# Wide one-hots of the counts, for eight groups of edges at a time, in a graph network kernel

## The chip, the cores and the metric

The kernel runs on one core of one Trainium2 chip. The metric is the device time of one execution in microseconds; the time of a kernel is the median of several runs. The engines of a core are named as in the profile: PE (TensorE, matrix products), with PEld for its loads of weights; DVE (VectorE); ACT (ScalarE); POOL (GpSimd, here the engine that issues gathers and scatters); SP (SyncE, here the engine that issues plain transfers). Each engine runs its own instructions in order and waits for the others by semaphores.

## The reference

A graph with 6,250 nodes of 256 features and 100,000 edges goes through four message-passing layers. The edges come sorted by `dst`.

```python
h = jnp.maximum(_layernorm(x, axis=-1), 0.0)      # the input of the network
def agg(h):
    return jax.ops.segment_sum(h[src], dst, num_segments=N)
x1 = h
for l in range(NL - 1):                            # three layers
    g = x1 + agg(x1)
    g = jax.nn.relu(g @ W1s[l] + b1s[l])
    g = jax.nn.relu(g @ W2s[l] + b2s[l])
    x1 = g @ W3s[l] + b3s[l]
g = x1 + agg(x1)                                   # the head
g = jax.nn.relu(g @ cW1 + cb1)
g = jax.nn.relu(g @ cW2 + cb2)
return x + g @ cW3 + cb3
```

## The kernel before

The 6,250 nodes are `NT` = 49 blocks of 128. The sum over edges is a matrix product: for a block of 128 destination nodes a matrix of counts (source nodes x 128 destinations, entries "so many edges from here to there") multiplies the feature rows. The counts are small, so a matrix is kept as bytes, and the product `agg` (L1928) takes it block by block of sources, with the features split into a rounded part and a remainder (`XY`, two matmuls for each half of the features). The matrices depend on the edges alone: they are built once, during layer 0, stored to memory (`mats`) and read again by the later layers. `BUILT` = 32 destination blocks ("slots") have such a matrix. The other work of a layer, up to 19 blocks of destinations, goes by gathers: POOL fetches rows of the feature table by index (L1613) and DVE adds them up (`sums`, L1649; the first pair of rows of a block is copied by ACT, L1645). Behind either comes the small network of the layer (L1408, L1505).

**How counts are built.** 32 slots x 2 halves x 4 make 256 *units*, one more for a long block. A unit (`BATCH` = 4 groups of 128 edges; a group has at most 128 edges, one a partition, whose destinations are four neighbouring nodes) makes two one-hots in bfloat16:

- `lo`, 128 x (4 x 128): for each edge, a 1 at the lane of its source node within a block. One DVE operation for the four groups (L1197), which compares `lanes` with the edges' codes. The codes are held doubled in `pairs` (each twice, side by side), a copy that ACT makes for 16 groups at a time (L1190).
- `hi`, 128 x (4 x 98): for each edge, at the column of its source block (49 blocks x 2), a weight. The two columns of a block hold a 16-bit number each, that is two counts of a byte; the weight says which byte the edge adds to. Four DVE operations, one a group (L1215): compare `cols` with the edge's column code and multiply by its weight, both scalars of the partition, read from `marks`, float32 copies that ACT makes for 16 groups at a time (L1192).

PE multiplies `lo` by `hi` group by group (L1245, four matmuls into `bp`), and ACT (now and then DVE) casts `bp` into `at`, the bytes of the slot (L1253, L1255); SP stores a finished slot (L1261).

**What sets the order.** The program is written out in order by Python generators, with no scheduler behind it. `build` yields once a unit. The first `PRE` = 28 units (three slots and four units) are built alone, between them the steps of `listed`, which sorts the blocks of nodes and, with `at` of L1728, makes the list of edges that POOL fetches (L1734) for the gathers. Six of its steps are one-hot products of their own (L1702, L1706, L1711 on DVE, L1718 on PE). Then `product` runs over panels of up to four slots and 49 blocks of sources; at each step it emits the DVE and ACT work that is due, units of `build` by a table of goals (`goals`, about one a step at first), and the four `agg` matmuls, whose operand `a` is cast from bytes by ACT or DVE some steps ahead (L1896 to L1901). While unit k is emitted, `lo` and `hi` of unit k + 1 are emitted ahead of it, and the codes of the unit four further on. `lo`, `hi` and `bp` have two buffers each, so `lo` of unit k + 1 waits for the matmuls of unit k - 1. Gathers are released by time estimates that advance with PE's matmuls (`passed`). Layer 0 ends near 720 us of the span; nothing is built after it.

Of the kernel before, what the change touches and what calls it, by code (L numbers as in the profile page):

```python
# [9 lines left out]
F32 = mybir.dt.float32  # L10
# [4 lines left out]
BF16 = mybir.dt.bfloat16  # L15
AF = mybir.ActivationFunctionType
OP = mybir.AluOpType
PSUM = bass.MemoryType.PSUM
DRAM = bass.MemoryType.DRAM
P = 128  # L20
# [400 lines left out]
def sorted_edges(  # L421
# [39 lines left out]
    nc = tc.nc  # L461
# [10 lines left out]
    GSUB = 64 // GD  # L472
    TWO = GD // 2
    HW = NT * TWO
# [4 lines left out]
    BATCH = 4  # L479
# [52 lines left out]
    clT = const.tile([P, 3, GSUB, 2 * BUILT], BF16, name="clT")  # L532
# [7 lines left out]
    extra = const.tile([P, 3, BATCH], BF16, name="extra")  # L540
    limit = const.tile([P, NS], F32, name="limit")
    mark = const.tile([1, 4], F32, name="mark")
    cT, weigh, loT = clT[:, 0], clT[:, 1], clT[:, 2]
    colf = const.tile([P, P], F32, name="colf")
    cols = const.tile([P, HW], BF16, name="cols")
    lanes = const.tile([P, P], BF16, name="lanes")
# [550 lines left out]
    with tc.manual_schedule():  # L1097
        with tc.tile_pool(name="prep", bufs=2) as prep, tc.tile_pool(
            name="ps_t", bufs=2, space=PSUM
# [67 lines left out]
        batches = []  # L1167
# [5 lines left out]
                batches.append((slot, None, 1, GSUB - BATCH))  # L1173
        hot = {}

        pairs, marks = {}, {}

        def pair(hots, k):

            if k < len(batches):  # L1180
                slot, s, half, q0 = batches[k]
                if s is None:
                    pairs[slot, 2] = hots.tile([P, BATCH, 2], BF16, name="more", bufs=1)
                    nc.vector.tensor_copy(pairs[slot, 2],
                                          extra[:, 2, :, None].to_broadcast([P, BATCH, 2]))
                    marks[slot, 2] = hots.tile([P, 2, BATCH], F32, name="moremarks", bufs=1)
                    nc.vector.tensor_copy(marks[slot, 2], extra[:, :2])
                elif q0 == 0:
                    pairs[slot, half] = hots.tile([P, GSUB, 2], BF16, name="pairs", bufs=3)
                    nc.scalar.copy(pairs[slot, half], loT[:, :, s, None].to_broadcast([P, GSUB, 2]))  # L1190
                    marks[slot, half] = hots.tile([P, 2, GSUB], F32, name="marks", bufs=3)
                    nc.scalar.copy(marks[slot, half], clT[:, :2, :, s])  # L1192

        def one_hot(o, values, which, n):

            shape = [P, BATCH, n // 2, 2]
            nc.vector.tensor_tensor(  # L1197
                o.rearrange("p q (n t) -> p q n t", t=2),
                values.rearrange("p (n t) -> p n t", t=2)[:, None, :, :].to_broadcast(shape),
                which[:, :, None, :].to_broadcast(shape), OP.is_equal)  # L1200

        def low_hot(hots, k):
            if k < len(batches):
                slot, s, half, q0 = batches[k]
                lo = hots.tile([P, BATCH, P], BF16, name="lo", bufs=2)
                one_hot(lo, lanes, pairs[slot, 2] if s is None else pairs[slot, half][:, q0:q0 + BATCH], P)
                hot[k] = [lo]

        def high_hot(hots, k):
            if k < len(batches):  # L1210
                slot, s, half, q0 = batches[k]
                hi = hots.tile([P, BATCH, HW], BF16, name="hi", bufs=2)
                w, o = (marks[slot, 2], 0) if s is None else (marks[slot, half], q0)
                for q in range(BATCH):
                    nc.vector.tensor_scalar(hi[:, q, :], cols, w[:, 0, o + q:o + q + 1],  # L1215
                                            w[:, 1, o + q:o + q + 1], op0=OP.is_equal, op1=OP.mult)
                hot[k].append(hi)

        own_at = [None]

        def build(hots, ats, ps_b):


            each = GSUB // BATCH
            pair(hots, 0)
            low_hot(hots, 0)
            high_hot(hots, 0)
            step, held = 0, None
            for k, (slot, s, half, q0) in enumerate(batches):
                if half == 0 and q0 == 0:  # L1230
                    at = own_at[0] = ats.tile([P, NT, P], U8, name="at", bufs=2)
                more = k + 1 < len(batches) and batches[k + 1][1] is None
                sets = [hot.pop(k)] if held is None else [held, hot.pop(k)]
                pair(hots, k + each)
                if s is not None:
                    low_hot(hots, k + 1)
                    high_hot(hots, k + 1)
                if more:
                    held = sets[0]
                    yield  # L1240
                    continue
                bp = ps_b.tile([P, W], F32, name="bp")
                for m in range(BATCH):
                    for i, (lo, hi) in enumerate(sets):
                        mm = nc.tensor.matmul(bp[:, m * HW:(m + 1) * HW], lo[:, m, :], hi[:, m, :],  # L1245
                                              start=(i == 0), stop=(i == len(sets) - 1))
                passed(SLOW if now[0] < PRE else BUILD * len(sets), mm)
                d = (half * 64 + q0 * GD) // 2
                o = at.bitcast(U16)[:, :, d:d + BATCH * TWO].rearrange("p h (i d) -> p h i d", i=BATCH)
                v = bp[:, :BATCH * HW].rearrange("p (i h d) -> p h i d", i=BATCH, d=TWO)  # L1250
                step += 1
                if step % 8 or step <= PRE:
                    nc.scalar.copy(o, v)  # L1253
                else:
                    nc.vector.tensor_copy(o, v)  # L1255
                if half and q0 + BATCH == GSUB:
                    kind, b = seq[slot]
                    if kind == "u":
                        own = at[:, b - NS, :]
                        nc.vector.tensor_tensor(own, own, ident, OP.add)  # L1260
                    nc.sync.dma_start(out=mats[slot // 4][:, slot % 4, :],  # L1261
                                      in_=at.rearrange("p h d -> p (h d)"))
                if s is None:
                    held = None
                    low_hot(hots, k + 1)
                    high_hot(hots, k + 1)
                yield

        CH = 7
# [602 lines left out]
        def passed(t, ins=None):  # L1872

            clock[0] += t
            if ins is not None:
                paced[:] = [ins.ins.name]
                for g in layers:
                    g.flow()
# [85 lines left out]
        with tc.tile_pool(name="hots", bufs=1) as hots, tc.tile_pool(  # L1964
            name="ats", bufs=1
        ) as ats, tc.tile_pool(name="rings", bufs=AHEAD + 2) as rings, tc.tile_pool(
            name="gath", bufs=9
        ) as gath, tc.tile_pool(name="nd", bufs=1) as nd, tc.tile_pool(
            name="ps_a", bufs=2, space=PSUM
        ) as ps_a, tc.tile_pool(name="ps_b", bufs=2, space=PSUM) as ps_b:  # L1970
            begun = {0: clock[0]}
            beside = build(hots, ats, ps_b)
            lists = listed(nd, ps_b)
            while now[0] < PRE:
                next(beside)
                built[0] += 1
                next(lists, None)
                tick(layers[0])
                layers[0].advance()
                if built[0] == UNITS * (FIRST - 1) + 3:  # L1980
                    at = chunks.tile([P, 4, CH * P], U8, name="at", bufs=5)
                    nc.sync.dma_start(out=at[:, :FIRST - 1, :], in_=mats[0][:, :FIRST - 1, :CH * P])
                if built[0] == UNITS * FIRST:
                    mat[0, 0] = [(at[:, :FIRST - 1, j * P:(j + 1) * P], own_at[0][:, j, :])
                                 for j in range(CH)]
                    for _ in range(2):
                        fetch(0, 0)
            for p in range(last[0] + 1):
                product(0, p, ps_a, beside)
            assert next(beside, None) is None and built[0] == total  # L1990
            assert next(lists, 0) == 0
# [14 lines left out]
def kernel(  # L2006
# [27 lines left out]
    rest = (x, src, dst, W1s, b1s, W2s, b2s, W3s, b3s, cW1, cb1, cW2, cb2, cW3, cb3, out)  # L2034
    earlier = []
    sorted_edges(tc, good, earlier, *rest)
    done = nc.values_load(good[0:1, 0:1], min_val=0, max_val=1)
    with tc.If(done == 0):
# [27 lines left out]
```

## Time and profile before

| What | Value |
|---|---|
| Median of 3 runs | 2024.81 us (2024.36 to 2026.46) |
| The profiled execution | 2030.06 us |
| Its span, first to last instruction | 2028.2 us |
| PE busy | 1909.6 us, 94% |
| DVE busy | 1118.4 us, 55% |
| `hi`, L1215, 1024 operations | 250.7 us of DVE |
| `lo`, L1197, 256 operations | 107.0 us of DVE |

All times of the trace are of one profiled execution, counted from the start of its span. A row of the page's slices has 40 digits, one for 50.7 us each, in tenths of busy time. In a timeline, a row is the start, the duration, the engine, the line and operation, what is written and read with the sizes, and in brackets how long the engine was idle before it and whose work ended that; neighbouring rows of one kind are merged (x4), with the duration from the start of the first to the end of the last. In a table of stretches each engine has its busy time and, behind it, the number of instructions, then the granted clock of PE (1.00 is full), the share of the DMA engines, and GB/s. A row of the list of waits gives who waited for whom, the total in microseconds, how often, and the longest.

### The profile page before, as it was taken

To read this page: it belongs to the slowest core of one execution; us is meant where nothing else is said; L and a number is where in the kernel's file an instruction comes from. 1 tells how busy PE (TensorE), PEld (TensorE's weight loads), DVE (VectorE), ACT (ScalarE), POOL (GpSimd) and SP (SyncE) were. 2 spreads that over 40 slices of the span, in tenths; PEclk is the share of its full clock that TensorE was granted. 3 is DMA by queue.
4 is the path that set the end of the run, shared out by engine and by line. 5 is a ranking of instruction groups with operands and counts; after the bars stand their busy time and mean duration, and the time that the engine had idled before them with its cause. 6 is when DMAs were issued, how large, how long until landed. Compare 5 with 4: busy or idle time off the path is not lost. (4 is left out here: it accounts for less than half of the span.)

```text
span 2028.2 us, 29980 instructions
## 1 busy us (share of the span) xinstructions
PE 1909.6 (94%) x9236; PEld 1477.3 (73%) x9236; DVE 1118.4 (55%) x2984; ACT 1080.1 (53%) x2228; POOL 1304.6 (64%) x1444
## 2 busy tenths in 40 slices
PE   5856999999999899999999999999999999999997
PEld 3643667677777777777789777777789777777765
DVE  7779989898876634334344443333335344443433
ACT  4634667676676555444444564444445464454442
POOL 2525556666766637677777656776777466777775
PEclk9876999999999999999999999999999999999998
DMA  5513546666656746556556675555557576665553
GB/s 167 172 59 121 166 148 210 198 203 188 208 175 192 227 151 191 171 180 184 170 174 189 195 225 172 169 169 179 179 173 214 160 233 191 197 190 178 181 174 106
DMA packets 252342, 361.47 MB, mean 178 GB/s; under 512 B 33353, under 2 KB 206313, under 8 KB 252155
## 3 DMA queue, kind: packets, MB, share of 16 engines
q1 hardware_dynamic: 188160, 190.34, 29.7%
q0 software_dynamic: 61952, 166.87, 27.6%
q10 hardware_dynamic: 2058, 2.25, 0.4%
q8 instruction: 74, 1.21, 0.3%
q14 instruction: 98, 0.79, 0.1%
HBM read 292.33 MB, written 67.40 MB: 177 GB/s over the span
## 5 line engine op out<-in xcount | busy, mean ns | idle before, releaser
L1928 PE MATMUL agg<-a,XY 128*128 128x512 f32 (+1 forms) x6272 | 1510.7, 393 | 16.0 <-DVE a L1901 9.6
L1613 POOL DMA_INDIRECT rows<-table,idxN x1121 | 1084.0, 967 | 493.5 <-PE agg L1928 205.8
L1928 PEld LDWEIGHTS agg<-a,XY 128*128 128x128 f32 x6272 | 1144.3, 189 | 254.6 <-issue 15.0
L1899 ACT CAST a<-at 128x512 fp32r<-128x512 uint8 (+1 forms) x1249 | 707.4, 601 | 239.6 <-PE agg L1928 228.9
L1649 DVE TENSOR_TENSOR sums<-sums,rows 128x512 f32<-128x512 f32 x477 | 333.1, 698 | 483.9 <-DMA rows<-table,idxN 441.7
L1215 DVE TENSOR_SCALAR hi<-cols,marks 128x98 bf16<-128x98 bf16 x1024 | 250.7, 326 | 0.0
L1901 DVE CAST a<-at 128x512 fp32r<-128x512 uint8 (+1 forms) x312 | 141.2, 459 | 167.4 <-PE agg L1928 141.9
L1253 ACT CAST at<-bp 128x392 uint16<-128x392 f32 x227 | 111.0, 489 | 144.6 <-PE bp L1245 141.6
L1245 PE MATMUL bp<-hi,lo 128*128 128x98 bf16 x1028 | 118.7, 215 | 34.9 <-DVE hi L1215 31.5
L1245 PEld LDWEIGHTS <-lo 128*128 128x128 bf16 x1028 | 61.3, 100 | 111.1 <-DVE hi L1215 65.7
L1408 PE MATMUL ps<-h,w 128*128 128x512 f32 (+2 forms) x336 | 135.8, 548 | 0.0
L1505 PE MATMUL ps<-w,h 128*128 128x256 f32 x588 | 133.7, 379 | 0.0
L1197 DVE TENSOR_TENSOR lo<-lanes,pairs 128x512 bf16<-128x512 bf16 x256 | 107.0, 418 | 29.7 <-PE bp L1245 25.1
L1505 PEld LDWEIGHTS ps<-w,h 128*128 128x128 f32 x588 | 111.2, 190 | 15.8
L596 POOL DMA_INDIRECT table<-zz,ids x72 | 72.1, 1002 | 68.8 <-DVE zz L1510 48.4
L1645 ACT COPY sums<-rows 128x512 f32<-128x512 f32 x74 | 43.8, 592 | 123.8 <-DMA rows<-table,idxN 93.7
L1411 ACT ACTIVATE h<-ps,bias 128x512 f32<-128x512 f32 (+2 forms) x84 | 51.7, 636 | 96.0 <-PE ps L1408 95.8
L1510 DVE TENSOR_TENSOR zz<-ps,w 128x512 f32<-128x512 f32 (+1 forms) x81 | 50.4, 637 | 94.5 <-PE ps L1505 87.5
L1408 PEld LDWEIGHTS ps<-h,w 128*128 128x128 f32 x336 | 63.1, 193 | 52.4 <-issue 37.3
L1684 ACT ACTIVATE h<-pt,bias 128x256 f32<-128x256 f32 (+1 forms) x84 | 33.1, 446 | 126.6 <-PE pt L1676 125.3
L1335 DVE TENSOR_TENSOR XY<-back,XY 128x256 fp32r<-128x256 f32 x138 | 54.1, 421 | 42.5 <-ACT XY L1334 41.9
L1942 ACT ACTIVATE h<-agg,bias 128x512 f32<-128x512 f32 (+1 forms) x60 | 37.3, 670 | 73.5 <-PE agg L1928 73.3
(235 smaller groups left out, 889.3 us busy)
## 6 DMA issues: line engine op xcount, KB each, us to landing
at<-mat SPq DMA_DIRECT2D x140, 448.0 KB
mat<-at SPq DMA_DIRECT2D x32, 784.0 KB
at<-mat SPq DMA_DIRECT2D x62, 336.0 KB
rows<-table,idxN POOLq DMA_INDIRECT x1121
back<-table SPq DMA_DIRECT2D x138, 128.0 KB
table<-zz SPq DMA_DIRECT2D x35, 256.0 KB
at<-mat SPq DMA_DIRECT2D x63, 112.0 KB
own<-zz SPq DMA_DIRECT2D x55, 128.0 KB
```

Source lines behind the costliest of these rows:

```text
L596: got = nc.gpsimd.indirect_dma_start(out=ap, out_offset=bass.IndirectOffsetOnAxis(ap=ids[:, b:b + 1], axis=0), in_=sb, in_offset=None)
L1197: nc.vector.tensor_tensor(o.rearrange("p q (n t) -> p q n t", t=2), values.rearrange("p (n t) -> p n t", t=2)[:, None, :, :].to_broadcast( ...
L1215: nc.vector.tensor_scalar(hi[:, q, :], cols, w[:, 0, o + q:o + q + 1], w[:, 1, o + q:o + q + 1], op0=OP.is_equal, op1=OP.mult)
L1245: mm = nc.tensor.matmul(bp[:, m * HW:(m + 1) * HW], lo[:, m, :], hi[:, m, :], start=(i == 0), stop=(i == len(sets) - 1))
L1253: nc.scalar.copy(o, v)
L1408: mm = nc.tensor.matmul(ps[:, :w], weights[l][0][:, c, i * P:(i + 1) * P], h1[:, c, :w], start=(c == 0), stop=(c == KC - 1))
L1505: mm = nc.tensor.matmul(o, h2[0][:, c, nodes], w3[:, c, :], start=(c == 0), stop=(c == KC - 1))
L1613: got = nc.gpsimd.indirect_dma_start(out=t[:, c % 2, :], out_offset=None, in_=tables[self.l][:, :], in_offset=bass.IndirectOffsetOnAxis(ap ...
L1649: nc.vector.tensor_tensor(sums, sums, rows.rearrange("p h c -> p (h c)"), OP.add)
L1899: nc.scalar.copy(o, v)
L1901: nc.vector.tensor_copy(o, v)
L1928: mm = nc.tensor.matmul(agg[c][:, :w], XY[:, j, o:o + P], a[:, :w], start=(i == 0 and half == 0), stop=(i == NT - 1 and half == 1))
```

## The change

`hi` is made for two units, eight groups, at once: one comparison of `cols` with the eight groups' column codes, and one multiplication, in place, by their weights. For this the codes and weights too are held doubled, in one tile with those of `lo`: `pairs` becomes 3 x 16 x 2 in bfloat16 and `marks` goes. `high_hot` is called in every second unit, for the units two and three ahead; it then makes the entry of `hot` to which `low_hot` adds. A helper, `compare`, does all three operations; `of` gives the number of groups: eight, or four for the long block's extra unit.

```diff
         def pair(hots, k):
...
                 elif q0 == 0:
-                    pairs[slot, half] = hots.tile([P, GSUB, 2], BF16, name="pairs", bufs=3)
-                    nc.scalar.copy(pairs[slot, half], loT[:, :, s, None].to_broadcast([P, GSUB, 2]))
-                    marks[slot, half] = hots.tile([P, 2, GSUB], F32, name="marks", bufs=3)
-                    nc.scalar.copy(marks[slot, half], clT[:, :2, :, s])
+                    pairs[slot, half] = hots.tile([P, 3, GSUB, 2], BF16, name="pairs", bufs=3)
+                    nc.scalar.copy(pairs[slot, half],
+                                   clT[:, :, :, s, None].to_broadcast([P, 3, GSUB, 2]))
...
+        def compare(o, values, which, op):
+
+            n, width = o.shape[1], o.shape[2]
+            shape = [P, n, width // 2, 2]
+            o = o.rearrange("p q (n t) -> p q n t", t=2)
+            if values is None:
+                values = o
+            else:
+                values = values.rearrange("p (n t) -> p n t", t=2)[:, None, :, :].to_broadcast(shape)
+            nc.vector.tensor_tensor(o, values, which[:, :, None, :].to_broadcast(shape), op)
...
         def high_hot(hots, k):
             if k < len(batches):
-                slot, s, half, q0 = batches[k]
-                hi = hots.tile([P, BATCH, HW], BF16, name="hi", bufs=2)
-                w, o = (marks[slot, 2], 0) if s is None else (marks[slot, half], q0)
-                for q in range(BATCH):
-                    nc.vector.tensor_scalar(hi[:, q, :], cols, w[:, 0, o + q:o + q + 1],
-                                            w[:, 1, o + q:o + q + 1], op0=OP.is_equal, op1=OP.mult)
-                hot[k].append(hi)
+                codes, o, n = of(k)
+                hi = hots.tile([P, 2 * BATCH, HW], BF16, name="hi", bufs=2)
+                compare(hi[:, :n], cols, codes[:, 0, o:o + n], OP.is_equal)
+                compare(hi[:, :n], None, codes[:, 1, o:o + n], OP.mult)
+                for i in range(n // BATCH):
+                    hot[k + i] = [hi[:, i * BATCH:(i + 1) * BATCH]]
...
                 if s is not None:
                     low_hot(hots, k + 1)
-                    high_hot(hots, k + 1)
+                    if q0 % (2 * BATCH) == 0:
+                        high_hot(hots, k + 2)
```

DVE's order before, in the part built alone, from the last one-hots of `listed` to `at` of L1728 (x4 stands for four equal instructions; a semaphore that is waited for is named in brackets, Activation for ACT):

```order
L1711 TENSOR_TENSOR moved<-block,what 128x576 [waits DVE_49]
L1197 TENSOR_TENSOR lo<-lanes,pairs 128x512 [waits PE_49]
L1215 TENSOR_SCALAR hi<-cols,marks 128x98 x4
L1197 TENSOR_TENSOR lo<-lanes,pairs 128x512 [waits PE_49]
L1215 TENSOR_SCALAR hi<-cols,marks 128x98 x4
L1197 TENSOR_TENSOR lo<-lanes,pairs 128x512 [waits PE_49]
L1215 TENSOR_SCALAR hi<-cols,marks 128x98 [waits DVE_49]
L1215 TENSOR_SCALAR hi<-cols,marks 128x98 x3
L1723 COPY got<-sums 128x144 [waits PE_49]
L1725 SCALAR_TENSOR_TENSOR begin<-got 128x24 [waits DVE_49]
L1728 SCALAR_TENSOR_TENSOR at<-got,begin 128x24 [waits DVE_49]
```

And the same place of the changed kernel, with its own line numbers (L1200 is the operation in `compare`; L1720, L1732 and L1737 are L1711, L1723 and L1728 of before):

```order
L1720 TENSOR_TENSOR moved<-block,what 128x576 [waits DVE_49]
L1200 TENSOR_TENSOR lo<-lanes,pairs 128x512 [waits PE_49]
L1200 TENSOR_TENSOR hi<-cols,pairs 128x784
L1200 TENSOR_TENSOR hi<-hi,pairs 128x784 [waits DVE_49]
L1200 TENSOR_TENSOR lo<-lanes,pairs 128x512 [waits PE_49] x2
L1200 TENSOR_TENSOR hi<-cols,pairs 128x784 [waits Activation_49]
L1200 TENSOR_TENSOR hi<-hi,pairs 128x784 [waits DVE_49]
L1732 COPY got<-sums 128x144 [waits PE_49]
L1734 SCALAR_TENSOR_TENSOR begin<-got 128x24 [waits DVE_49]
L1737 SCALAR_TENSOR_TENSOR at<-got,begin 128x24 [waits DVE_49]
```

Twelve narrow `hi` have become two wide pairs, two `lo` stand next to each other, and the multiplication waits for the comparison. From the first one-hot up to L1728, 16 `lo` and 64 `hi` stand in the kernel before, 14 `lo` and 9 pairs of wide operations in the changed one.

On ACT, the copies ahead of the first casts of `bp`, before:

```order
L1190 COPY pairs<-clT 128x32
L1192 CAST marks<-clT 128x32
L1253 CAST at<-bp 128x49x8 [waits PE_49] x4
L1190 COPY pairs<-clT 128x32
L1192 CAST marks<-clT 128x32
```

and changed (L1188 is the copy, L1262 the cast of L1253):

```order
L1188 COPY pairs<-clT 128x96
L1262 CAST at<-bp 128x49x8 [waits PE_49] x4
L1188 COPY pairs<-clT 128x96
L1262 CAST at<-bp 128x49x8 [waits PE_49] x4
L1188 COPY pairs<-clT 128x96 [waits DVE_49,Activation_49]
```

One copy of 96 elements stands in the place of two of 32. The instructions of PE, POOL and SP and their order are the same in both kernels.

More of the change, by code (lines that the diff above doesn't have):

```diff
@@ L1174, in sorted_edges @@
         hot = {}
-        pairs, marks = {}, {}
+        pairs = {}
         def pair(hots, k):
@@ L1182, in pair @@
                 if s is None:
[L1183 to L1187, printed above, removed]
-                elif q0 == 0:
-                    pairs[slot, half] = hots.tile([P, GSUB, 2], BF16, name="pairs", bufs=3)
-                    nc.scalar.copy(pairs[slot, half], loT[:, :, s, None].to_broadcast([P, GSUB, 2]))
-                    marks[slot, half] = hots.tile([P, 2, GSUB], F32, name="marks", bufs=3)
-                    nc.scalar.copy(marks[slot, half], clT[:, :2, :, s])
@@ L1194, in one_hot @@
[L1194 to L1200, printed above, removed]
+                    pairs[slot, 2] = hots.tile([P, 3, BATCH, 2], BF16, name="more", bufs=1)
+                    nc.vector.tensor_copy(pairs[slot, 2], extra[:, :, :, None].to_broadcast(
+                        [P, 3, BATCH, 2]))
+                elif q0 == 0:
+                    pairs[slot, half] = hots.tile([P, 3, GSUB, 2], BF16, name="pairs", bufs=3)
+                    nc.scalar.copy(pairs[slot, half],
+                                   clT[:, :, :, s, None].to_broadcast([P, 3, GSUB, 2]))
@@ new lines, in compare, with of @@
+        def compare(o, values, which, op):
[7 more added lines that the diff above has]
+            nc.vector.tensor_tensor(o, values, which[:, :, None, :].to_broadcast(shape), op)
+        def of(k):
+            slot, s, half, q0 = batches[k]
+            if s is None:
+                return pairs[slot, 2], 0, BATCH
+            assert q0 % (2 * BATCH) == 0
+            return pairs[slot, half], q0, 2 * BATCH
@@ L1205, in low_hot @@
                 lo = hots.tile([P, BATCH, P], BF16, name="lo", bufs=2)
-                one_hot(lo, lanes, pairs[slot, 2] if s is None else pairs[slot, half][:, q0:q0 + BATCH], P)
-                hot[k] = [lo]
+                codes, o = (pairs[slot, 2], 0) if s is None else (pairs[slot, half], q0)
+                compare(lo, lanes, codes[:, 2, o:o + BATCH], OP.is_equal)
+                hot[k].append(lo)
         def high_hot(hots, k):
             if k < len(batches):
-                slot, s, half, q0 = batches[k]
-                hi = hots.tile([P, BATCH, HW], BF16, name="hi", bufs=2)
-                w, o = (marks[slot, 2], 0) if s is None else (marks[slot, half], q0)
-                for q in range(BATCH):
-                    nc.vector.tensor_scalar(hi[:, q, :], cols, w[:, 0, o + q:o + q + 1],
-                                            w[:, 1, o + q:o + q + 1], op0=OP.is_equal, op1=OP.mult)
-                hot[k].append(hi)
+                codes, o, n = of(k)
[4 more added lines that the diff above has]
+                    hot[k + i] = [hi[:, i * BATCH:(i + 1) * BATCH]]
         own_at = [None]
@@ L1225, in build @@
             pair(hots, 0)
+            high_hot(hots, 0)
             low_hot(hots, 0)
-            high_hot(hots, 0)
             step, held = 0, None
@@ L1243, in build @@
                 for m in range(BATCH):
-                    for i, (lo, hi) in enumerate(sets):
+                    for i, (hi, lo) in enumerate(sets):
                         mm = nc.tensor.matmul(bp[:, m * HW:(m + 1) * HW], lo[:, m, :], hi[:, m, :],
@@ L1264, in build @@
                     held = None
+                    high_hot(hots, k + 1)
                     low_hot(hots, k + 1)
-                    high_hot(hots, k + 1)
                 yield
```

## The prediction

> **What bounds the kernel now.** First the page: its span, the share of each engine, and the slices.
>
> ```profile
> span 2028.2 us, 29980 instructions
> ...
> PE 1909.6 (94%) x9236; PEld 1477.3 (73%) x9236; DVE 1118.4 (55%) x2984; ACT 1080.1 (53%) x2228; POOL 1304.6 (64%) x1444
> ...
> PE   5856999999999899999999999999999999999997
> ...
> DVE  7779989898876634334344443333335344443433
> ```
>
> TensorE (PE) is the bound over nearly all of the span. VectorE (DVE) is full only in the early slices, and only there can the change, which touches DVE and two small ACT copies, move the end. Next, busy time by stage.
>
> ```profile
> core 0: us, PE busy (x) PEld busy (x) DVE busy (x) ACT busy (x) POOL busy (x), PEclk, DMA share, GB/s
> 135.00:183.00 48.00, 26.86 (x136) 12.15 (x136) 47.30 (x177) 16.85 (x48) 13.29 (x14) 0.52 0.24 77
> 183.00:199.00 16.00, 13.44 (x80) 10.66 (x80) 13.34 (x57) 8.03 (x23) 12.15 (x13) 0.85 0.60 178
> 199.00:259.00 60.00, 53.56 (x321) 40.41 (x321) 58.97 (x226) 39.69 (x99) 34.11 (x36) 0.94 0.52 160
> 259.00:300.00 41.00, 38.20 (x311) 26.13 (x310) 34.21 (x159) 23.10 (x51) 19.84 (x22) 1.00 0.49 153
> 300.00:400.00 100.00, 99.54 (x555) 71.06 (x554) 90.50 (x303) 71.86 (x157) 63.78 (x68) 1.00 0.62 194
> ```
>
> The third column is DVE. It is saturated in 135 to 183 (the one-hots built alone) and in 199 to 259 (beside the first product); 183 to 199 is something else, below. From 300 on PE is full and DVE has room. PE's 53.56 busy in 199 to 259 hides idling: four build matmuls whose operands are there take 0.35 us, four that come one by one behind DVE take 0.85, as the timeline shows.
>
> ```profile
> 200.32 0.85 PE L1245 MATMUL bp<-hi,lo 128*128 128x98 bf16 x4 [1.49 <-DVE hi L1215]
> ...
> 209.48 0.35 PE L1245 MATMUL bp<-hi,lo 128*128 128x98 bf16 x4
> 209.66 0.95 PE L1928 MATMUL agg<-a,XY 128*128 128x384 f32 x4
> 210.45 0.88 PE L1245 MATMUL bp<-hi,lo 128*128 128x98 bf16 x4
> ```
>
> A fed unit (four build matmuls, four of the product) takes PE 210.45 - 209.48 = 0.97 us. The stretch holds 36 units (count below), so PE needs some 35 of its 60 us, and DVE sets the pace. How DVE spends a unit:
>
> ```profile
> 160.44 0.42 DVE L1197 TENSOR_TENSOR lo<-lanes,pairs 128x512 bf16<-128x512 bf16 x1
> 160.77 0.95 DVE L1215 TENSOR_SCALAR hi<-cols,marks 128x98 bf16<-128x98 bf16 x4
> ...
> 161.64 0.42 DVE L1197 TENSOR_TENSOR lo<-lanes,pairs 128x512 bf16<-128x512 bf16 x1
> ```
>
> From start to start `lo` costs 0.33 and its four `hi` operations 0.87: 1.20 us a unit, 1.74 for eight `hi`.
>
> **Price of the new operations.** No row shows a 128x784 operation. The nearest:
>
> ```profile
> L1197 DVE TENSOR_TENSOR lo<-lanes,pairs 128x512 bf16<-128x512 bf16 x256 | 107.0, 418 | 29.7 <-PE bp L1245 25.1 <-ACT pairs L1190 3.0 <-ACT a L1899 0.9
> L1711 DVE TENSOR_TENSOR moved<-block,what 128x576 bf16<-128x576 bf16 x6 | 4.5, 758 | 0.2
> L1702 DVE TENSOR_TENSOR lane<-lanes,goal 128x512 bf16<-128x512 bf16 x6 | 4.1, 682 | 0.0
> ...
> 137.68 0.68 DVE L1702 TENSOR_TENSOR lane<-lanes,goal 128x512 bf16<-128x512 bf16 x1
> 138.28 0.25 DVE L1706 TENSOR_TENSOR block<-lanes,goal 128x96 bf16<-128x96 bf16 x1
> 138.57 0.76 DVE L1711 TENSOR_TENSOR moved<-block,what 128x576 bf16<-128x576 bf16 x1
> 139.25 0.42 DVE L1197 TENSOR_TENSOR lo<-lanes,pairs 128x512 bf16<-128x512 bf16 x1
> ```
>
> (Timeline rows have start, duration, engine and line; in the grouped ones above them the two numbers behind the first bar are busy us and mean ns of one.) `block`, `lane` and `moved`, whose code is one number spread along a row, take 0.25, 0.68 and 0.76 us at 96, 512 and 576 elements, which 149 ns + 1.04 ns an element fits. `lo`, whose codes are doubled so that neighbours differ in memory, costs 418 at 512: the same 149 and half the slope. The new operations double their codes as `lo` does, so I take 149 + 0.52 x 784 = 557 ns each. The ends are 418 (a wider operation is not cheaper than `lo`) and 149 + 1.04 x 784 = 965 (full slope). The multiplication reads what the comparison wrote: `moved` starts 0.04 after the end of `block`, on which it depends; the independent `lo` starts 0.08 before `moved` ends. So eight groups cost 0.557 + 0.04 + 0.475 = 1.07 us instead of 1.74; with two `lo`, two units take 1.73 instead of 2.40, or 0.335 less a unit. At the ends the eight cost 0.79 or 1.89.
>
> **The change, stage by stage.** The counts of units are those of `lo`, by stretch:
>
> ```profile
> core 0: us, DVE busy (x), PEclk, DMA share, GB/s
> 135.00:164.00 29.00, 6.67 (x16) 0.53 0.13 51
> 135.00:183.00 48.00, 12.04 (x29) 0.52 0.24 77
> 183.00:199.00 16.00, 3.35 (x8) 0.85 0.60 178
> 199.00:259.00 60.00, 14.93 (x36) 0.94 0.52 160
> 259.00:300.00 41.00, 6.25 (x15) 1.00 0.49 153
> 300.00:690.00 390.00, 70.84 (x169) 1.00 0.63 197
> ```
>
> *135 to 199.* Here 37 units would give 12.4 us, but not all of it counts, because a chain on POOL with its own pace ends the stretch:
>
> ```profile
> 164.59 0.18 DVE L1728 SCALAR_TENSOR_TENSOR at<-got,begin 128x24 int32<-128x24 f32 x1
> 165.63 0.98 POOL L1734 DMA_INDIRECT lane<-padded,at  x1 [31.29 <-DVE hi L1215]
> 188.23 0.95 POOL L1734 DMA_INDIRECT lane<-padded,at  x1 [0.30 <-DMA lane<-padded,at]
> 189.48 0.95 POOL L1613 DMA_INDIRECT rows<-table,idxN  x1 [0.30 <-PE bp L1245]
> 196.26 0.59 ACT L1645 COPY sums<-rows 128x512 f32<-128x512 f32 x1 [2.98 <-DMA rows<-table,idxN]
> 197.72 0.34 PE L1245 MATMUL bp<-hi,lo 128*128 128x98 bf16 x4 [1.34 <-ACT at L1253]
> ```
>
> Once DVE has written `at`, POOL asks for the edges of 19 tiles, 1.25 us apart, then for rows; the first two rows land at 196.26, 31.5 us after `at`. ACT waits there in order, with the casts of `bp` and `a` behind it, so PE and then DVE wait. That chain is as long after the change. What counts is how much earlier DVE reaches `at`: before it come 16 units, 16 x 1.20 = 19.2 us; in the new order 14 `lo` and 9 wide pairs, 14 x 0.33 + 9 x 1.07 = 14.3. Gain 4.9 us. The other 7.5 turn into a longer wait of ACT at L1645, some 10 us instead of 2.98. PE's clock suffers from such waits (the column PEclk has 0.85 in 183 to 199, 1.00 from 259 on), so I charge 1 us.
>
> *199 to 259.* 36 x 0.335 = 12.0 us, inside the 25 that PE has to spare.
>
> *259 to 300.* PE is nearly full, but in some units still meets its `hi` one by one after DVE's own wait for PE at L1836:
>
> ```profile
> PE bp L1245 <- DVE hi L1215: 2.7, 8, 0.8
> ```
>
> With `hi` made two units ahead only `lo` is left in that path: I take the 2.7 us.
>
> *From 300.* PE is full; the 169 units left give DVE and not PE time: nothing. What hides the wide operations is DVE's tenth of idle time and two `lo` buffers. ACT's 32-element copies merge into one of 96 elements, hidden with the ACT time saved. The orders of PE, POOL and SP do not change, so no queue is passed and no wait added; DVE's new wait, of the multiplication for the comparison, is in the 1.07.
>
> Sum: 4.9 - 1.0 + 12.0 + 2.7 = 18.6 us off the profiled execution of 2030.06 us. That one stands 5.25 above the median of 2024.81, from which I subtract the same: **2006**. The uncertainty by which a measurement tells from no change is about 0.2%, 4 us.
>
> **Rivals.**
>
> 1. *The chain on POOL does not hold the start* (the stall is made up by what ran ahead). Then all 12.4 us of the first stretches count: 26 off, 1999. Against it: ACT's order is fixed and PE has two `bp`. With the low price of 0.79, 199 to 259 would give 18 x 0.95 = 17 and the sum is also near 26. Chance 0.09.
>
> 2. *Part of the gain is given back.* In 199 to 259 DVE runs into row transfers or ACT casts and half of the 12 is lost, 2012; or the multiplication in place alone costs 965, eight groups 1.48, and the terms become 1.3 + 4.7 + 2.7, 2016. No row shows a doubled-code multiplication. Chance 0.18.
>
> 3. *The width costs what the count saves.* At 965 each, eight groups take 1.89 for 1.74: `at` comes 2.4 later, 199 to 259 grows by 18 x 0.15 = 2.7, and the 2.7 of 259 to 300 may go or stay: 2027 to 2030. It decides from 890 ns an operation. Against: `lo` has the same layout at 418. Chance 0.06. The Trainium skill, VectorE: DVE Perf Modes, section on the perf-mode tier table, speaks against the change more strongly: bf16 `tensor_scalar` runs at four elements a cycle and `tensor_tensor` at two. By that rate alone (an estimate at the page's 0.96 GHz) eight narrow operations would stream 0.20 us and the two wide ones 0.82, and 27 wide pairs would end near 2041. The trace differs: a narrow `hi` takes 0.87 / 4 = 0.22 us from start to start for 98 elements, hardly any of it by the element.
>
> 4. *The burst starves PE* (slower). A wide pair holds DVE for 1.07 us at one go; where sums and casts of `a` stand behind it, the next `lo` may be late, in the full stretch from 300 on. There are 169 / 2 = 84 pairs; from 18.6 / 84 = 0.22 us lost a pair the change is a loss, and at 0.3 the time is 2031. Against it, the timeline of that stretch:
>
> ```profile
> 406.01 0.95 DVE L1215 TENSOR_SCALAR hi<-cols,marks 128x98 bf16<-128x98 bf16 x4
> ...
> 408.03 0.35 PE L1245 MATMUL bp<-hi,lo 128*128 128x98 bf16 x4
> ```
>
> The operands lie ready from 406.96, a good microsecond before their use, and the change takes DVE time away. Chance 0.05.
>
> **How the numbers follow.** The forecast case holds 0.62: 2001 to 2011, its terms a few microseconds either way. The range reaches to rival 1 below and rival 2 above: 1999 to 2016, leaving out rivals 3 and 4 and the edges. Faster by over 0.2%: the forecast and rivals 1 and 2, 0.89; rival 3 splits between same and slower, rival 4 is mostly slower: same 0.04, slower 0.07.
>
> **What would show it.** Right: wide operations near 557 ns, two units of `lo` and `hi` in about 1.73 us while the one-hots are built alone, `at` about 5 us earlier, a wait of about 10 us at the first `sums` copy on ACT, that copy again 31.5 us after `at`, and PE's idle time behind `hi` gone before 300. Wrong: wide operations near 965; no wait at that copy; or PE idle behind `lo` after 300.

## The result, and the profile after

The changed kernel takes 2006.57 us, the median of 6 runs (2004.85 to 2012.81), beside 2025.45 us for the kernel before in 6 runs of the same session (2022.87 to 2026.86). The ratio is 0.9911, with a 95% interval of 0.9897 to 0.9925: 18.9 us faster, where the prediction had 18.6 and 2006. Its profiled execution took 2005.61 us. The page:

```profile
span 2003.8 us, 29049 instructions
...
PE 1885.4 (94%) x9236; PEld 1472.8 (74%) x9236; DVE 1034.1 (52%) x2213; ACT 1077.4 (54%) x2164; POOL 1311.1 (65%) x1444
...
PE   5955999999999899999999999999999999999997
...
DVE  7877887677756343333344353333345354343433
```

DVE has 84 us less to do, and its early slices are no longer nines. PE still bounds the rest. The groups of the one-hots, with their mean duration in ns behind the busy time:

```profile
L1200 DVE TENSOR_TENSOR lo<-lanes,pairs 128x512 bf16<-128x512 bf16 x256 | 107.1, 424 | 45.1 <-PE bp L1254 44.3
...
L1200 DVE TENSOR_TENSOR hi<-hi,pairs 128x784 bf16<-128x784 bf16 x128 | 72.6, 568 | 4.4
L1200 DVE TENSOR_TENSOR hi<-cols,pairs 128x784 bf16<-128x784 bf16 x128 | 72.0, 562 | 3.1 <-ACT pairs L1188 3.1
```

The comparison takes 562 ns and the multiplication 568; 557 was worked out for both. In the part that is built alone, the timeline of DVE just ahead of `at` of L1737 (the list that POOL fetches edges by):

```profile
157.03 0.76 DVE L1200 TENSOR_TENSOR lo<-lanes,pairs 128x512 bf16<-128x512 bf16 x2
157.69 0.56 DVE L1200 TENSOR_TENSOR hi<-cols,pairs 128x784 bf16<-128x784 bf16 x1
158.29 0.57 DVE L1200 TENSOR_TENSOR hi<-hi,pairs 128x784 bf16<-128x784 bf16 x1
158.78 0.30 DVE L1732 COPY got<-sums 128x144 f32<-128x144 f32 x1
...
159.33 0.18 DVE L1737 SCALAR_TENSOR_TENSOR at<-got,begin 128x24 int32<-128x24 f32 x1
```

Two units take 158.78 - 157.03 = 1.75 us (1.73 in the prediction, 2.40 before). Then the chain that starts at `at`, on POOL, ACT, PE and DVE:

```profile
160.37 1.50 POOL L1743 DMA_INDIRECT lane<-padded,at  x1 [27.24 <-DVE spot L1754]
185.74 0.95 POOL L1622 DMA_INDIRECT rows<-table,idxN  x1 [0.31 <-DMA lane<-padded,at]
189.83 0.59 ACT L1654 COPY sums<-rows 128x512 f32<-128x512 f32 x1 [7.11 <-DMA rows<-table,idxN]
191.30 0.49 PE L1254 MATMUL bp<-hi,lo 128*128 128x98 bf16 x4 [5.44 <-ACT at L1262]
191.57 1.63 PE L1937 MATMUL agg<-a,XY 128*128 128x384 f32 x4
192.36 0.70 DVE L1658 TENSOR_TENSOR sums<-sums,rows 128x512 f32<-128x512 f32 x1 [6.89 <-DMA rows<-table,idxN]
```

The wait that was 2.98 us on ACT is now 7.11 us, and PE (5.44 idle) and DVE (6.89 idle) stand behind it: what DVE saved beyond `at` is spent there. The next stretches:

```profile
core 0: us, PE busy (x) PEld busy (x) DVE busy (x) ACT busy (x) POOL busy (x), PEclk, DMA share, GB/s
192.60:244.40 51.80, 47.27 (x327) 38.40 (x326) 46.48 (x118) 39.00 (x91) 34.97 (x35) 0.93 0.59 186
...
290.00:390.00 100.00, 99.58 (x550) 70.34 (x549) 71.53 (x149) 70.68 (x144) 65.57 (x70) 1.00 0.65 204
```

The first is what took the 60 us from 199 to 259 before. DVE, full then, has 5.3 of 51.8 us idle. From 290 on PE is as full as it was, and DVE has dropped from 90.50 to 71.53 of 100.

### The profile page after: what moved, and what is told of

It reads as the page before. It is cut to its first block, busy times and chain, and to the rows that moved or that the text cites. A ratio compares the mean times of both kernels' runs of the same rounds, so it can differ in the third digit from the quotient of the medians.

```text
span 2003.8 us, 29049 instructions
## 1 busy us (share of the span) xinstructions
PE 1885.4 (94%) x9236; PEld 1472.8 (74%) x9236; DVE 1034.1 (52%) x2213; ACT 1077.4 (54%) x2164; POOL 1311.1 (65%) x1444
## 4 chain that ended last, share of the span: by engine, by line
PE 83%; DVE 6%; DMA 4%; issue 2%; POOL 2%; ACT 1%; SPq 0%; DVEq 0%; ACTq 0%; POOLq 0%
PE agg L1937 66%; PE ps L1514 6%; PE ps L1417 6%; DMA rows<-table,idxN 2%; PE bp L1254 2%; POOL rows L1622 1%; DVE hi L1200 1%; PE pt L1685 1%; PE bp L1046 1%; DVE lo L1200 1%; POOL lane L1743 1%; PE ps L1431 1%; DMA wd<-joined,starts 0%; DVE ws L768 0%; DMA lane<-padded,at 0%
## 5 line engine op out<-in xcount | busy, mean ns | idle before, releaser
L1262 ACT CAST at<-bp 128x392 uint16<-128x392 f32 x227 | 110.3, 489 | 128.0 <-PE bp L1254 122.2
L1200 DVE TENSOR_TENSOR lo<-lanes,pairs 128x512 bf16<-128x512 bf16 x256 | 107.1, 424 | 45.1 <-PE bp L1254 44.3
L1254 PE MATMUL bp<-hi,lo 128*128 128x98 bf16 x1028 | 95.2, 219 | 33.4 <-DVE lo L1200 27.1
L1514 PEld LDWEIGHTS ps<-w,h 128*128 128x128 f32 x588 | 111.2, 190 | 15.9
L1200 DVE TENSOR_TENSOR hi<-hi,pairs 128x784 bf16<-128x784 bf16 x128 | 72.6, 568 | 4.4
```

The lines of the kernel that those rows point to most:

```text
L1200: nc.vector.tensor_tensor(o, values, which[:, :, None, :].to_broadcast(shape), op)
L1514: mm = nc.tensor.matmul(o, h2[0][:, c, nodes], w3[:, c, :], start=(c == 0), stop=(c == KC - 1))
```

## The path of the gain

PE issues the same 9236 matmuls in the same order in all the kernels here, so the n-th matmul of two traces can be compared. The table gives by how much a kernel's trace is ahead of that of the kernel before, at the matmuls that stood at these times before. The difference in when the first one-hot starts is taken off: the preparation ahead of it, which the change does not touch, ended anywhere between 132.6 and 136.7 us in these executions.

| Kernel | 197.7 (first after the wait) | 259 | 300 | 400 | 600 |
|---|---|---|---|---|---|
| predicted | 3.9 | 15.9 | 18.6 | 18.6 | 18.6 |
| changed kernel, three executions | 5.3, 5.4, 5.3 | 13.7, 13.8, 13.4 | 17.2, 17.3, 16.3 | 18.1, 18.2, 17.3 | 17.9, 18.0, 17.1 |
| e1, four groups wide | 4.2 | 9.7 | 11.0 | 12.0 | 11.8 |
| e2, narrow, made ahead | -2.9 | -0.9 | 1.4 | 0.9 | 0.0 |
| e5, edges in many parts | 5.9 | 14.3 | 16.3 | 17.2 | 17.0 |
| e8, last edges later | 6.5 | 16.3 | 20.7 | 21.7 | 21.5 |
| e6b, codes not doubled | -5.4 | -6.2 | -4.7 | -6.2 | -11.6 |
| e7b, no multiplication | 10.6 | 23.0 | 28.6 | 29.6 | 29.7 |

After 600, at the end of layer 0, every kernel here gains another 4 to 6 us on this one trace of before, the slower e6b too. Most of this has a cause in the traces. From 300 to 700 PE of the kernel before waits four times for `hi`, all of them near 619 and near 684:

```profile
PE bp L1245 <- DVE hi L1215: 2.6, 4, 1.2
```

DVE had waited there for rows, 4.16 us at the first place, and still had to make the `hi` that PE needed next. In the three traces of the changed kernel, in e2 and in e7b, which all make `hi` two units ahead, this wait is not there, and their lead grows by 1.8 to 1.9 us at each of the two places, by 3.6 to 3.8 from 600 to 690; e1, one unit ahead, gets 1.4. The last 2 us, between 700 and 720, stay open: there is one trace of before, and its execution stood 5.25 above its median.

## Experiments

The theory: the gain is DVE's operations saved before 300 us, at half the price an element because the codes are doubled, and the chain on POOL caps its first part. Rivals: it comes from making `hi` two units ahead, whatever the operations cost; it comes from ACT's merged copies; the chain is no cap. The changed kernel ran with each of the two main sets, as a control.

> The changed kernel again, as the yardstick of the runs beside it: 2006 to 2007 us, ratio to the kernel before 0.991. Theory 1 (DVE sets the pace until some 300 us, a chain on POOL caps the first part of the gain, PE carries the rest on unchanged): the trace shows ACT waiting some 7 us at the first sums copy, and the lead over the kernel before falls by some 4 us there.

Measured in the first set: 2006.09 us (before 2027.37), ratio 0.9894 [0.9879, 0.9909].

> The changed kernel, as the yardstick of the three runs beside it: 2006 to 2007 us where the kernel before takes 2025, ratio 0.990 to 0.991.

Measured in the last set: 2007.74 us (before 2026.99), ratio 0.9907 [0.9893, 0.9920].

### The order alone (e2)

The narrow operations of before, but eight at once and two units ahead, as the changed kernel has them.

```diff
+                hi = hots.tile([P, 2 * BATCH, HW], BF16, name="hi", bufs=2)
+                n = BATCH if s is None else 2 * BATCH
+                for q in range(n):
+                    nc.vector.tensor_scalar(hi[:, q, :], cols, w[:, 0, o + q:o + q + 1],
+                                            w[:, 1, o + q:o + q + 1], op0=OP.is_equal, op1=OP.mult)
```

> The narrow operations of the kernel before, in the order of the changed one: eight of them at once, two units ahead. Theory 1: DVE's work is the same, so only the waits behind L1836 go, 1 to 4 us, 2021 to 2024 us. The rival that the order (hi two units ahead) makes the gain expects 2007 to 2012.

Measured: 2022.65 us, ratio 0.9978 [0.9969, 0.9987]. So the order is worth 4.7 us of the 21.3 that the changed kernel gains in this set. The table shows a loss first (eight narrow operations in a row make `at` come 31.1 us after the first one-hot, 29.3 before) and a slow recovery to 300. At 600 us nothing is left of the lead (0.0); the 3.8 us that the trace gains by 690 come at 619 and 684. So the time came out near the expected one, but not the place: the stretch of the waits behind L1836, 259 to 300, gives 2.3 us, and the other stretches together take them back. What PE waits for most between 190 and 260 us of this trace is no longer `hi` but `lo`:

```profile
PE bp L1248 <- DVE lo L1197: 9.3, 12, 1.6
```

Making `hi` ahead does not remove a wait for a full DVE; it moves it to the operation that is left.

### Half the width (e1)

Wide operations over the four groups of one unit, one unit ahead.

```diff
-            return pairs[slot, half], q0, 2 * BATCH
+            return pairs[slot, half], q0, BATCH
...
+                    high_hot(hots, k + 1)
                     low_hot(hots, k + 1)
-                    if q0 % (2 * BATCH) == 0:
-                        high_hot(hots, k + 2)
```

> Wide operations over the four groups of one unit (two operations of 392 elements a unit), one unit ahead as in the kernel before. Theory 1 prices them by the fixed cost and the slope: 149 + 0.52 x 392 = 353 ns each, 0.67 us a unit in place of 0.87, a gain of 0.20 a unit where the full change has 0.335: some 3 us at the edge list, some 6 in 199 to 259, 1 to 2 behind L1836, 2014 to 2016 us. A rival that puts the gain down to making hi two units ahead expects 2020 us or more; a rival that puts it down to being free of the operations per group, whatever the width, expects 2007.

Measured: 2016.35 us, ratio 0.9948 [0.9935, 0.9962]. The groups:

```profile
L1200 DVE TENSOR_TENSOR hi<-hi,pairs 128x392 bf16<-128x392 bf16 x256 | 93.0, 363 | 8.8
L1200 DVE TENSOR_TENSOR hi<-cols,pairs 128x392 bf16<-128x392 bf16 x256 | 91.9, 359 | 46.4 <-PE bp L1252 40.9 <-ACT pairs L1188 3.1 <-ACT a L1906 1.1
```

From 392 to 784 elements the comparison grows by 203 ns, 0.52 an element, and 156 ns are fixed. Half the width leaves half the gain, 11.0 of 21.3 us, 0.35 us above the range expected. The other 10.3 are not the fixed part alone, because e1 also makes `hi` only one unit ahead: the order by itself gave 4.7 in e2. If the two add up, which no run shows, 5.6 are left for a fixed part paid half as often.

### Codes not doubled (e6b)

The same wide operations, with one code spread along a row.

```diff
+            if n > BATCH or width == HW:
+                nc.vector.tensor_tensor(o.rearrange("p q n t -> p q (n t)"),
+                                        values.rearrange("p q n t -> p q (n t)"),
+                                        which[:, :, 0:1].to_broadcast([P, n, width]), op)
```

> The wide operations with each code spread along its row, a second time, beside the changed kernel. The first time the operations took 0.97 us as priced, but the kernel stayed 11 us under the kernel before on a chip on which every kernel took 10% longer. Theory 1 with the operations of e2_narrow_ahead (hi two units ahead is worth some 4 us by itself): 1.89 for 1.74 us for eight groups costs some 5 us, the order gives 4 back, 2022 to 2028 us, about 20 above the changed kernel. If the number of operations counts by itself, 2010 to 2016.

Measured: 2036.35 us, ratio 1.0051 [1.0038, 1.0065], 9 us slower than before; a miss of the size. The price is the one expected:

```profile
L1201 DVE TENSOR_TENSOR hi<-cols,pairs 128x784 bf16<-128x784 bf16 x128 | 124.3, 971 | 3.1 <-ACT pairs L1188 3.1
L1201 DVE TENSOR_TENSOR hi<-hi,pairs 128x784 bf16<-128x784 bf16 x127 | 123.8, 975 | 4.3
```

By 300 us the kernel is 4.7 us behind, about the cost worked out, and the 4 us that the order was to give back are not there. It loses as much again between 400 and 600, where PE was taken to be out of reach. The waits of PE and of its weight loads, from 284 to 684 us, in this kernel:

```profile
PE bp L1259 <- DVE lo L1205: 7.1, 9, 1.4
```

```profile
PEld L1259 <- DVE lo L1205: 21.0, 42, 1.9
```

And in the changed one, where PE itself never waits for `lo` in this stretch:

```profile
PE agg L1937 <- ACT h L1951: 1.3, 4, 0.3
```

```profile
PEld L1254 <- DVE lo L1200: 7.5, 26, 0.6
```

A pair that holds DVE for 1.9 us at one go makes the next `lo` late for a weight load by up to 1.9 us, more than the microsecond or so that lay ready before. DVE as a whole is no fuller than in the kernel before (87.8 us of 100 over 310 to 610, 87.6 over 300 to 600 there), so the load does not explain it. This is the burst of rival 4, at nearly twice the pair that the changed kernel has; at 1.09 us the longest such wait is 0.6 and the table is flat from 400 to 600.

### Without the multiplication (e7b)

```diff
                 compare(hi[:, :n], cols, codes[:, 0, o:o + n], OP.is_equal)
-                compare(hi[:, :n], None, codes[:, 1, o:o + n], OP.mult)
```

> Without the multiplication by the weights (that part of the computation left out), a second time, beside the changed kernel: theory 1 still expects DVE to be the bound in a part of the first 300 us, 5 to 9 us under the changed kernel; a change under 2 us would say that DVE has stopped being the bound.

Measured: 1993.96 us, ratio 0.9847 [0.9832, 0.9861], 13.8 us under the changed kernel of the same set: more than expected. Of this 11 to 12 us lie before 300 (the table's 28.6 against 16.3 to 17.3). `at` comes 20.2 us after the first one-hot instead of 25.2 and the whole chain moves with it, 5.3 us at the wait; the two stretches behind give 4 and 2 us more. DVE still sets the end before 300, although it is idle a tenth of the time: its idle time lies where its rows or PE's matmuls are late, not where PE waits for `lo`.

### The edges in other portions (e5, e8)

In e5 POOL asks for the edges of the first 8 of the 19 blocks, and for the others between the requests for rows. In e8 it asks for 15 first, and for the last four later.

```diff
+            def fetch_set(i):
+                for b0, n in nodes_of[0][i:i + 1]:
+                    for b in range(b0, b0 + n):
+                        fetch(run[:, starts_of[b]:starts_of[b] + wide_of[b]], wide_of[b], b)
+
+            fetch_set(0)
+            fetch_set(1)
...
+                    if step == 2:
+                        fetch_set(nodes_of[0].index((b0, n)) + 2)
```

> The changed kernel, with the edges of the first 8 of 19 blocks asked for at first and those of the later ones in later steps, so that the first gathers of rows don't stand behind all 19 requests on POOL. Theory 1 says that these requests cap the first part of the gain: the wait of ACT at the first sums copy falls from 7 us to 2 or less, and 3 to 5 us more are gained, 2001 to 2003 us. If the wait has another cause, or is made up for later, the time stays at 2006 to 2007.

Measured: e5 2005.61 us, ratio 0.9891 [0.9876, 0.9906], not to be told from the changed kernel; a miss. The first `sums` copy no longer waits, but DVE does, for edges that are now asked for behind rows:

```profile
182.25 0.60 ACT L1654 COPY sums<-rows 128x512 f32<-128x512 f32 x1
...
188.58 0.26 DVE L1768 SCALAR_TENSOR_TENSOR some<-lane,spot,some 128x42 f32<-128x42 int32 x1 [4.21 <-DMA lane<-padded,at]
189.51 0.51 PE L1254 MATMUL bp<-hi,lo 128*128 128x98 bf16 x4 [3.83 <-DVE lo L1200]
```

POOL has the same 19 requests to make; which engine stands waiting for the next one is all that changed. Hence the milder e8:

```diff
+            for i in range(4):
+                fetch_set(i)
...
+                    if step == 2:
+                        i = nodes_of[0].index((b0, n)) + 3
+                        fetch_set(i if i > 3 else len(nodes_of[0]))
```

> The changed kernel, with the edges of the first 15 of 19 blocks asked for ahead of the gathers of rows and those of the last 4 between them. In e5_fetch_split the wait left the first sums copy on ACT and came back on DVE, for edges asked for too late. Theory 1 (POOL's requests cap the first part): the first rows stand 4 requests, 5 us, earlier, no edges come late, so ACT's wait of 7 us falls to 2 or 3 and 3 to 5 us are gained, 2001 to 2004 us. If another wait takes its place again, 2005 to 2007.

Measured: 2001.97 us, ratio 0.9879 [0.9864, 0.9894], 5.8 us under the changed kernel of the same set, the time expected; the two intervals just touch, so the difference is only just told from noise. The wait on ACT, which was to fall to 2 or 3 us, fell to 5.74:

```profile
180.99 0.95 POOL L1622 DMA_INDIRECT rows<-table,idxN  x1 [0.30 <-PE bp L1254]
...
188.98 0.59 ACT L1654 COPY sums<-rows 128x512 f32<-128x512 f32 x1 [5.74 <-DMA rows<-table,idxN]
...
189.68 0.70 DVE L1658 TENSOR_TENSOR sums<-sums,rows 128x512 f32<-128x512 f32 x1 [3.70 <-ACT sums L1654]
```

Rows are asked for 21.2 us after `at` instead of 26.4, but the copy gains only 1.3 us (29.2 us after `at` instead of 30.5), since these rows land 8.0 us after their first request, 4.1 in the changed kernel. DVE restarts without waiting for the second pair. The table has 1.2 us more at the wait, and 2.3 more by 300. So the chain is a cap, and part of it is the transfer of the rows itself.

### ACT's copies (e3)

The changed kernel with an extra copy of 32 elements kept on ACT.

```diff
+                    marks = hots.tile([P, 2, GSUB], BF16, name="marks", bufs=1)
+                    nc.scalar.copy(marks, clT[:, :2, :, s])
```

> The changed kernel, with a second 32-element copy on ACT for each 16 groups again, as the copy of marks in the kernel before (its result is not used). Theory 1: ACT has room there, no change, 2006 to 2008 us. A rival that puts a part of the gain down to the 64 ACT copies that went expects 2010 us or more.

Measured: 2200.27 us beside 2230.89 for the kernel before, ratio 0.9867 [0.9847, 0.9888]. This set ran on a chip on which every kernel took a tenth longer at a lower clock, so only its ratios are used. The gain is all there with the copy kept, so the merged copies did not make it, as far as a ratio from another chip can say: the changed kernel itself was not run on that chip. On it the kernel without the multiplication had 0.9833 [0.9812, 0.9854], about its later value, but the one with single codes 0.9949 [0.9933, 0.9966], the other sign than above, at the same 969 and 975 ns an operation. That is not explained. That DVE's bursts have more cover where PE is slower is a guess, which no run here tested.

## Why the prediction was right, point by point

**The sum, 18.6 us: 18.9 measured.** The mechanism held up to 300 us, but that the sum came out this close is luck. Against the traces one term was 1.4 too small, one 3.6 too large and one 0.8 too small, and behind 600, where nothing was forecast, PE gained 3.6 us more.

**135 to 199, +4.9 - 1.0 for PE's clock: 5.3 measured.** The mechanism holds: `at` earlier, then a chain of nearly the same length, then the same copy on ACT. Three sizes in it were off. `at` came 25.22 us after the first one-hot instead of 29.31, 4.1 earlier and not 4.9. The prediction, and the text ahead of it, counted 14 `lo` up to there in the changed kernel; the trace has 16 in both kernels, and 2 x 0.33 is most of the difference. The chain from `at` to the copy took 30.50 us instead of 31.67: POOL's requests took longer (26.4 instead of 24.9 to the first rows, below), but the rows landed 4.1 us after that request instead of 6.8. Why they landed sooner is open. And ACT's wait is 7.1, not some 10. The charge of 1 us for PE's clock rested on a mean of two clocks: in the kernel before the granted clock is 0.52 from 183 to 188 and 1.00 from 188 to 199, so the low part lay ahead of the wait, not behind it. In the changed kernel it is 0.50 behind the longer wait (191.3 to 193.5), but that falls into the next stretch.

**199 to 259, +12.0: 8.4 measured.** This term was over-sized. DVE's work fell as forecast, from 58.97 us to 46.48, 12.5 less. But DVE's idle time rose from 1.0 to 5.3 us, and 12.5 - 4.3 is 8.2. The waits of DVE and, by `hi` and `lo`, of the weight loads: first the changed kernel from 192.6 to 244.4, then the weight loads of the kernel before from 199 to 259:

```profile
DVE sums L1658 <- DMA rows<-table,idxN: 8.2, 2, 6.9
DVE lo L1200 <- PE bp L1254: 1.4, 3, 0.6
DVE at L1264 <- PE bp L1254: 0.6, 1, 0.6
```

```profile
PEld L1254 <- DVE lo L1200: 6.6, 18, 1.3
```

```profile
PEld L1245 <- DVE hi L1215: 10.0, 28, 1.8
```

The 6.9 is the stall ahead of 192.36; in the stretch itself DVE waits 1.3 us for rows and 2.0 for PE; the other 2 us of its idle time these rows don't name. The weight loads in turn still wait for `lo` 18 times, where they waited 28 times for `hi`. Behind the stall, at the low clock, the four `agg` matmuls at 191.57 took 1.63 us, against 0.94 at 196.89; but over the whole stretch the clock is 0.93, and 0.94 in the kernel before, so it is not what the term lacks. The step that failed is that DVE would run through this stretch without a gap. Rival 2, part of the gain given back here, happened in part: 3.6 of the 12.0, where it had half.

**259 to 300, +2.7: 2.9 to 3.5 measured.** Here the guess was a little low. The wait behind `hi` was the right place: PE no longer waits for `hi` there, and 0.6 us for `lo`.

**From 300, nothing: 0.7 measured to 600, then 3.6 or a little more at 619 and 684.** PE is full in both to 600, and no burst starves it. But "PE is full" was taken to hold to the end of the building. At 619 and 684 PE of the kernel before meets `hi` late after a wait of DVE's own, just as behind L1836, and two units ahead removes that too.

**The price, 557 ns: 562 and 568.** The slope of 0.52 was read off `lo`, whose layout the new operations share, and the slope of 1.04 off rows with a single code; e6b turned the one into the other. The row of the narrow `hi`, 218 ns from start to start for 98 elements, was trusted over the rates of the Trainium skill's tier table (VectorE: DVE Perf Modes, section on the perf-mode tier table), which would have had the change lose; the runs bear that out. These rates leave out what an operation costs beside its elements, 156 ns for the wide ones by e1; for the narrow ones no run varied the width. Rival 3 is excluded, rival 1 too (a stall of 7 us is there), and rival 4 at this width.

## What to carry to other kernels

Count what an operation costs beside its elements: 256 operations of 784 elements do in 145 us what 1024 of 98 did in 251, provided that the operand spread along the row changes in steps of two equal neighbours. When a full engine is relieved, work out the gain by stage, and allow for waits of that engine for its neighbours, which its fullness had hidden; here they took back about a third of the gain of the largest stage. Look also for the few places where a full engine meets its operand late: making it earlier was worth 3.6 us here at two of them, behind 600 us, where no gain was forecast. A cap by a chain on another engine is a sum of several links: asking 5.2 us earlier for the rows brought them only 1.3 us earlier.

## What the hardware showed that was not expected

POOL's requests for edges (`lane`, L1743 and its counterparts) take longer beside the wide operations. Per kernel, the minimum, median and largest duration in ns; before, the changed kernel, and e6b:

```profile
L1734 POOL DMA_INDIRECT lane<-padded,at x26: 943/947/1152, 165.6 to 254.4; - x26
```

```profile
L1743 POOL DMA_INDIRECT lane<-padded,at x26: 943/962/1504, 160.4 to 243.2; - x26
```

```profile
L1748 POOL DMA_INDIRECT lane<-padded,at x26: 940/1033/1692, 169.3 to 262.0; - x26
```

The 19 requests of the chain sum to 18.1 us before, 18.6 in e1, 18.8 in e2, 19.5 to 19.6 in the changed kernel and 21.8 in e6b. The length of DVE's wide operations with two inputs (361 ns in e1, 565 in the changed kernel, 973 in e6b) does not order them all, since e2 has the operations of the kernel before. What does is when a request begins. Two of them with the DVE operation that was under way, first in the changed kernel, then in e6b:

```profile
168.76 0.56 DVE L1200 TENSOR_TENSOR hi<-cols,pairs 128x784 bf16<-128x784 bf16 x1
...
168.80 1.34 POOL L1743 DMA_INDIRECT lane<-padded,at  x1 [0.30 <-issue]
```

```profile
181.66 0.97 DVE L1201 TENSOR_TENSOR hi<-hi,pairs 128x784 bf16<-128x784 bf16 x1
...
181.86 1.59 POOL L1748 DMA_INDIRECT lane<-padded,at  x1 [0.30 <-issue]
```

The first request ends 168.80 + 1.34 - 169.32 = 0.82 us after the DVE operation, and the second 181.86 + 1.59 - 182.63 = 0.82 us after its own. So it is, at 0.81 to 0.86 us, for all 13 of the 19 requests of e6b that begin within an operation with two inputs and at least 0.15 us ahead of its end, for 6 of 7 such requests in the changed kernel and for 4 of 5 in e2. The two others end that much after the next such operation. In the kernel before none of the 19 falls like this: most begin 0.22 us ahead of the end of a narrow `hi`, which reads one tile beside its two scalars, and take 0.94 to 0.98 us all the same. The Trainium skill, SBUF — State Buffer, section "Who interferes with whom", says that a DVE instruction with two inputs in SBUF contends with a GpSimd instruction that reads SBUF, and calls the ports that they share an exclusive lock; the numbers agree with that. The same section infers that such operations leave GpSimd's making of descriptors alone; for these requests, which read their indices from SBUF, the rows show that they are held up. Held up in this way, the chain became 1.5 us longer.
